# Where the first layer's projection stands, and how often it is halved, in two attention blocks in float32

## The chip, the cores and the metric

The kernel runs on one core of a Trainium2 chip. The metric is the device time of one execution in microseconds. PE is TensorE, DVE is VectorE, ACT is ScalarE, POOL is GpSimd, and SP is the engine whose queue issues most of the DMAs.

## The reference

There are 8 images of C = 512 channels and T = 1024 points, all in float32. Layer 0 has 8 heads of 64 channels, layer 1 has one head of 512.

```python
# layer 0
h = group_norm(x, 32 groups)
q, k, v = w_qkv @ h + b_qkv                       # 8 heads x 64
a = v @ softmax(k^T q / 8) , head by head
x = x + w_proj @ a + b_proj
# layer 1
h = group_norm(x, 8 groups)
q, k, v = q_w @ h + q_b, k_w @ h + k_b, v_w @ h + v_b
a = v @ softmax(q^T k / sqrt(512))
x = x + p_w @ a + p_b
```

## The kernel before

All products are float32 matmuls on PE. In layer 1 the weights of q and k are multiplied together once at the start (the product m) and so are those of v and p (the product z), so that an image needs g = m h, the scores h^T g, and z h times the exponentials.

**Halving.** A product of two matrices that are cut into quarters takes seven products of quarters in place of eight (Strassen's scheme in Winograd's form). `by_channel` and `by_token`, by way of `wino`, do this once: the seven factors of the image side are sums of halves of h (`image_factors`: eight differences of 128x512, in the tiles t1, t2, t4 and in place), those of the weights lie ready in DRAM (`keep`). `conv2` does it twice: each of the seven products is again cut into seven. For that the image side needs inner differences as well: `inner_factors` (line 414) makes 28 of 128x256, four for each of the seven outer factors. `conv2` goes through its products in four pairs (1 and 5; 2 and 6; 7; 3 and 4); each pair runs through the steps 1, 6, 2, 5, 7, 3, 4 (`inner_steps`), and what a pair leaves is added up further in the next. Evacuations out of PSUM are copies by ACT (lines 452 and 462) and additions by DVE (lines 528 and 530); a few additions between finished parts are made by POOL in SBUF (`more`, line 535).

The steps 3 and 4 of a pair, or of a whole `wino`, do not run at once. They stand in a list, `tail`, and the next pair or product runs its own step 1 first and then the list (`finish`). So PE has the tail of one product to do while ACT copies what the first step of the next one needs.

**Stages of image b, from 1 to 6, in PE's order:**

1. `attention0(b)`: eight units (four pairs of heads, two halves of the points). In each, PE makes scores, ACT exponentials (line 651), DVE their running sums (line 655), PE the product with v; ACT copies it to the tile a. The sums become reciprocals by way of DRAM (`reciprocals`) and a is multiplied by them (line 684). Between units, lists of hooks (`extra`) hold work for the next stage: the loads and the normalisation of layer 1's h of image b-1, its differences t by DVE, and a's own differences.
2. `projection(b)`: p = w_proj a, halved once, 28 matmuls of 512 columns. Meanwhile POOL makes the 28 inner differences of h1 of image b-1. Each evacuation adds the residual x on DVE (line 964); the result is stored to DRAM (`spill`), and its statistics for the second norm follow.
3. `layer1_scores(b-1)`: g by `conv2` with m.
4. `scores1`, then z by `by_token`, then `values1(b-1)`. In the hooks of `values1`, `factors_ahead` loads the next image's input, has ACT apply the first norm (`apply`, line 135, four instructions of 128x1024) and POOL make the inner differences of this h0.
5. `values(b+1)`: v by `conv2` with tokens in the rows. Ahead of it, the image after next is loaded (tiles `ahead`), and its statistics (line 93) are taken by DVE from a list, `background`, from which each step of a product takes one or a few entries.
6. `keys_and_queries(b+1)`: k and q, by `conv2`.

The first and the last image are framed somewhat differently. Weights go through three buffers in SBUF (`wpool`), loaded in the order of the list `uses`. Instructions with `keep_in_program_order` keep their place; the others may be moved on their engine by a scheduler. Each engine runs its own instructions strictly in order and waits on semaphores of the others.

Of the kernel before, what the change touches and what calls it, by code (L numbers as in the profile page):

```python
# [15 lines left out]
P = 128  # L16
EPS = 1e-5
ORDER = (1, 5, 2, 6, 7, 3, 4)
NBIG = 32
# [10 lines left out]
def two_attention_blocks_kernel(  # L30
# [22 lines left out]
    ident = const.tile([P, P], F32, name="ident")  # L53
    make_identity(nc, ident)
    ones = const.tile([P, P], F32, name="ones")
# [115 lines left out]
    def main_path(ctx):  # L171
# [7 lines left out]
        taken = []  # L179
        spool = ctx.enter_context(tc.tile_pool(name="spill", bufs=2, space=bass.MemoryType.DRAM))  # L180
# [111 lines left out]
        wdram2 = {n: dram.tile([P, 7, 7, P], F32, name=f"sums2_{n}") for n in "qkmv"}  # L292
# [21 lines left out]
        uses = ["p", *layer0] if B > 1 else ["p"]  # L314
        for b in range(1, B):
            uses += ["p", *twice["m"], "z"] + (layer0 if b + 1 < B else [])
# [86 lines left out]
        def inner_factors(hf, uid, pin=lambda ins: ins):  # L403

            f, steps = {}, []
            for p in ORDER:
# [5 lines left out]
                def make(ops=((t1, b12, b11), (t2, b22, t1), (t3, b22, b12), (t4, b21, t2))):  # L412
                    for dst, x, y in ops:
                        pin(nc.gpsimd.tensor_tensor(dst, x, y, ALU.subtract))  # L414
# [171 lines left out]
        def reciprocals(totals, uid, across, direct=None):  # L586
# [8 lines left out]
            for t in range(n):  # L595
                for i in range(4):
                    matmul(
                        sums[ts(i, 32), t, :, :], ones[:, :32], totals[t][:, :, ts(i, P)],
                        start=t == 0, stop=t == n - 1, skip_group_check=True,
                    )  # L600
# [31 lines left out]
        def attention0(b, q, k, v, a, extra):  # L632
# [3 lines left out]
            for hp in range(KC):  # L636
                for tb in (0, 1) if hp < KC - 1 else (1, 0):
# [35 lines left out]
                    if hp < KC - 1:  # L673
# [5 lines left out]
                    r = reciprocals(totals, uid, False, nc.scalar if (hp, tb) == (KC - 1, 0) else None)  # L679
                    totals = []  # L680
                    engine = nc.gpsimd if (b == 0 or hp == KC - 1) and (hp, tb) != (KC - 1, 0) else nc.vector
# [4 lines left out]
                    ]  # L686

            assert not extra
            return scaled[0]
# [118 lines left out]

        def natural(wt, nm, banks):
# [3 lines left out]
            for kc in range(KC):  # L813
                for o in range(KC):
                    transpose(pt[o][:, ts(kc, P)], wt[kc][:, ts(o, P)], ident)
# [36 lines left out]
        def prologue():  # L852
            raw_k = raw("k", 5)
# [46 lines left out]
            for n in "pz":  # L900
                t, steps = prepare(n)
                later.append(steps)
                later.append([lambda n=n, t=t: keep(n, t), load_weight])
# [86 lines left out]

        def norm_hooks(norm, uid):
# [16 lines left out]
        def keys_and_queries(b, f, norm, hooks):  # L1008
# [8 lines left out]
            else:  # L1017

                k = conv2("k", f, None, f"k0_{b}", [[all_background, *mean], [], [], affine])
                q = conv2("q", f, pcols("bq0"), f"q0_{b}")  # L1020
            return q, k

        def layer1_scores(b, inner):
            g = conv2("m", inner, ubias, f"g1_{b}")
# [29 lines left out]

        for b in range(B):
# [4 lines left out]
            h, loads, applies = [], [], []  # L1060
            if b > 0:
                h, loads, applies = begun(load_again, norm1, b - 1, "h1")
            elif B > 1:
                h, loads, applies = begun(load_x, norm0, 1, "h0")
            for f in loads:
# [3 lines left out]
            a = channel_tiles(f"a0_{b}")  # L1069

            here = lambda *t: tc.keep_in_program_order(nc.vector.tensor_sub(*t))
            af, steps = image_factors(a, f"a_{b}", here)

            if b > 0:
                hf, t = image_factors(h, f"h1_{b - 1}", here)
                for i, fs in enumerate((t[:1], t[1:2], (t[2], t[4]), (t[6], t[3]), (t[5], t[7]), steps[:2], steps[2:4])):
                    extra[2 * i + 3] += fs
            elif B > 1:
                hf, t = image_factors(h, "h0_1", here)
# [4 lines left out]
            if B > 1:  # L1084
                for f in steps[4:7]:
                    f()
            psum_pools(f"products_{b}", 2)
            xt = [load_x(b, c, "x") for c in range(KC)]
            if B > 1:

                inner, sums2 = inner_factors(hf, f"h1_{b - 1}" if b > 0 else "h0_1", tc.keep_in_program_order)
                for f in sums2:
                    f()
# [236 lines left out]
```

## Time and profile before

| | us |
|---|---|
| median of 3 runs | 2828.46 (2828.2 to 2830.94) |
| profiled execution | 2828.69 |
| its span | 2826.9 |
| period of a middle image (attention at 675.87, 1021.33) | 345.4 |
| projection p of that image, on PE | 792.62 to about 817.6 |
| g | from 817.62 |
| last product of layer 1 (`values1`) | 899.96 to 956.25 |
| v, k, q of the next image, from v's second step | 956.09 to 1021.26 |

The profile is of one execution. The mean clock granted to PE is 0.999 of the full one. A timeline's line has the start, the duration, the engine, the line of the kernel, the operation, out<-in by the tiles' names without their numbers, the shape, the count, and in brackets the idle time before it with what ended it. A float32 matmul of the program makes two records. Records overlap, so that PE's pace is read from starts.

### The profile page before, as it was taken

The page shows a single profiled execution, that of the slowest core. Times are in us where ns is not written, and L with a number is a line of the kernel's source. Part 1 is how long each engine was busy: PE and PEld are TensorE (multiplying, and loading weights), DVE is VectorE, ACT ScalarE, POOL GpSimd, SP SyncE. Part 2 cuts the span into 40 slices and gives each one's busy share as a digit, 9 for nine tenths or more (in the row PEclk, how much of TensorE's full clock was granted, in tenths as well). Part 3 has the DMA queues.
Part 4 walks back from the last instruction along what each step waited for, and adds up shares of the span by engine and source line. Part 5 has one row for each costly group of instructions (what it writes and reads, how often), then busy time and mean ns, then how long its engine had stood idle before and what let it go on. Part 6 is the DMA issues. An engine that isn't in the chain of part 4 may idle for free.

```text
span 2826.9 us, 33696 instructions
## 1 busy us (share of the span) xinstructions
PE 2808.6 (99%) x12434; PEld 1693.5 (60%) x12434; DVE 2005.0 (71%) x2833; ACT 942.7 (33%) x1205; POOL 1099.4 (39%) x1131
## 2 busy tenths in 40 slices
PE   9999999999999999999999999999999999999998
PEld 5435735866367653677537674376843868338584
DVE  5478677776777767777677766777667776676765
ACT  1252452214522145221552215422154312633130
POOL 2204205841057410664107730177202672036672
PEclk9999999999999999999999999999999999999999
DMA  8634303043031330323212232123311224112301
GB/s 285 209 114 151 147 17 127 27 174 139 24 139 52 147 129 17 139 98 120 110 50 105 101 138 90 53 102 122 140 67 53 102 112 159 36 58 90 119 5 72
DMA packets 107344, 292.41 MB, mean 103 GB/s; under 512 B 19171, under 2 KB 51235, under 8 KB 97446
## 3 DMA queue, kind: packets, MB, share of 16 engines
q1 hardware_dynamic: 105382, 287.92, 28.8%
q10 hardware_dynamic: 1792, 2.29, 0.3%
q8 instruction: 100, 1.64, 0.2%
q14 instruction: 70, 0.57, 0.1%
HBM read 237.47 MB, written 52.70 MB: 103 GB/s over the span
## 4 chain that ended last, share of the span: by engine, by line
PE 96%; DVE 2%; issue 1%; DMA 0%; POOL 0%; ACT 0%; DVEq 0%; ACTq 0%; POOLq 0%
PE sc L62 16%; PE av L62 15%; PE psb_av L62 6%; PE psb L62 5%; PE psa_av L62 4%; PE psc_av L62 4%; PE psc L62 3%; PE psa L62 3%; PE psb_z L62 3%; PE psb_k L62 3%; PE psb_g L62 3%; PE psb_v L62 3%; PE psb_p L62 3%; PE psb_q L62 2%; PE psa_z L62 2%; PE psc_z L62 2%
## 5 line engine op out<-in xcount | busy, mean ns | idle before, releaser
L655 DVE TENSOR_TENSOR sum<-sum,e 128x1024 f32<-128x1024 f32 x384 | 483.9, 1260 | 37.4 <-ACT e L651 0.5
L651 ACT ACTIVATE e<-sc 128x1024 f32<-128x1024 f32 x512 | 476.0, 1054 | 75.8 <-PE sc L62 74.2
L62 PE MATMUL sc<-q,k 64*128 64x512 f32 x2048 | 456.8, 596 | 0.0
L62 PE MATMUL av<-e,v 128*64 128x512 f32 x2048 | 453.6, 595 | 0.0
L684 POOL TENSOR_TENSOR a<-a,r 128x512 f32<-128x512 f32 (+1 forms) x11 | 20.0, 1817 | 903.3 <-DMA r<-all_rows 771.0
L62 PEld LDWEIGHTS sc<-q,k 64*128 64x128 f32 x2048 | 191.6, 186 | 248.0 <-issue 110.6
L62 PEld LDWEIGHTS av<-e,v 128*64 128x64 f32 x2048 | 141.3, 137 | 304.4 <-issue 292.3
L653 DVE TENSOR_TENSOR sum<-e,e 128x1024 f32<-128x1024 f32 x64 | 78.4, 1225 | 166.5 <-ACT e L651 166.5
L669 ACT COPY a<-av 128x512 f32<-128x512 f32 x64 | 37.5, 586 | 321.9 <-PE av L62 321.9
L62 PE MATMUL psb<-inner,inner_h 128*128 128x256 f32 x448 | 116.1, 382 | 0.9
L62 PE MATMUL psa_av<-e,z 128*128 128x512 f32 x256 | 113.3, 595 | 0.0
L414 POOL TENSOR_TENSOR inner_h<-h,inner_h 128x256 f32<-128x256 f32 x120 | 111.6, 931 | 3.5
L135 ACT ACTIVATE h<-h,b,s 128x1024 f32<-128x1024 f32 x62 | 78.5, 1270 | 87.1 <-DMA h<-in_x 69.4
L414 POOL TENSOR_TENSOR inner_h<-h 128x256 f32<-128x256 f32 x60 | 64.6, 1076 | 83.6 <-ACT h L135 83.6
L62 PEld LDWEIGHTS psb<-inner,inner_h 128*128 128x128 f32 x448 | 83.9, 190 | 16.6 <-POOL inner L429 3.5
L462 ACT COPY psb_v<-psa_v 128x512 f32<-128x512 f32 (+1 forms) x28 | 14.5, 517 | 222.4 <-DVE o L785 141.5
L725 POOL TENSOR_TENSOR sum<-sum,e 128x1024 f32<-128x1024 f32 x32 | 76.1, 2378 | 27.4 <-ACT e L721 26.1
L62 PE MATMUL psb_g<-inner_h,w_m 128*128 128x256 f32 x336 | 86.0, 383 | 0.3
L414 POOL TENSOR_TENSOR inner_h<-t_h,inner_h 128x256 f32<-128x256 f32 x90 | 84.2, 935 | 2.4
L414 POOL TENSOR_TENSOR inner_h<-t_h 128x256 f32<-128x256 f32 x90 | 79.9, 894 | 9.7 <-DVE t_h L165 9.7
L62 PEld LDWEIGHTS psa_av<-e,z 128*128 128x128 f32 x256 | 48.0, 190 | 57.3 <-issue 56.6
L721 ACT ACTIVATE e<-e 128x1024 f32<-128x1024 f32 x64 | 65.8, 1053 | 48.5 <-DVE e L711 26.2
(358 smaller groups left out, 5574.8 us busy)
## 6 DMA issues: line engine op xcount, KB each, us to landing
x<-in_x SPq DMA_DIRECT2D x36, 512.0 KB
h<-in_x SPq DMA_DIRECT2D x32, 512.0 KB
r<-all_rows SPq DMA_DIRECT2D x64, 256.0 KB
spill<-x SPq DMA_DIRECT2D x32, 512.0 KB
h<-spill SPq DMA_DIRECT2D x32, 512.0 KB
x<-spill SPq DMA_DIRECT2D x32, 512.0 KB
out<-x SPq DMA_DIRECT2D x64, 256.0 KB
w_p<-sums_p SPq DMA_DIRECT2D x8, 1792.0 KB
```

The lines of the kernel that those rows point to most:

```text
L62: tc.keep_in_program_order(nc.tensor.matmul(*args, **kw))
L135: tc.keep_in_program_order(nc.scalar.activation(dst, src, AF.Identity, bias=b, scale=s))
L414: pin(nc.gpsimd.tensor_tensor(dst, x, y, ALU.subtract))
L462: nc.scalar.copy(ps["b"], ps["a"])
L651: nc.scalar.activation(e, sc, AF.Exp, scale=(C // 8) ** -0.5)
L653: nc.vector.tensor_add(total, es[0], e)
L655: nc.vector.tensor_add(total, total, e)
L669: nc.scalar.copy(dst, av)
L684: engine.tensor_tensor(dst, dst, r, ALU.mult)
L721: nc.scalar.activation(e[c, cc, r], e[c, cc, r], AF.Exp, scale=scale)
L725: on = lambda dst, x, y: lambda: tc.keep_in_program_order(nc.gpsimd.tensor_tensor(dst, x, y, ALU.add))
```

## The change

For images 1 to 6:

- The projection leaves its place behind attention and stands between `values1(b-1)` and `values(b+1)`. It is halved twice (`projection2`, by `conv2`), for which the twice-halved sums of its weights are kept in DRAM too (`keep2`).
- Until then its input a waits in DRAM (`kept`): it is stored from attention pair by pair once it has been multiplied by the reciprocals, and loaded into the tiles `again` in the hooks of `values1`, where POOL makes its inner differences in the place where it made those of h0.
- The last two half units of attention have their reciprocals made together, and the last multiplication of a, by DVE, stands in g's second hook.
- The inner differences of h1 are made by DVE, in attention.
- The loads of h0 are issued behind `values1`'s code; its normalisation by ACT, its differences t and its inner differences by POOL stand in the hooks of the projection's four pairs.
- The residual is added by four separate additions of 128x1024 on DVE, in the hooks of v's first two pairs, and `spill` is stored behind them. The statistics of the second norm go to the background of k, and its means and factors to q.

There are 34 big tiles in place of 32; `ones` is narrower, and `ident` lies in a big tile. Images 0 and 7 keep the old way.

```diff
-NBIG = 32
+NBIG = 34
...
-        wdram2 = {n: dram.tile([P, 7, 7, P], F32, name=f"sums2_{n}") for n in "qkmv"}
+        wdram2 = {n: dram.tile([P, 7, 7, P], F32, name=f"sums2_{n}") for n in "qkmvp"}
...
-        uses = ["p", *layer0] if B > 1 else ["p"]
-        for b in range(1, B):
-            uses += ["p", *twice["m"], "z"] + (layer0 if b + 1 < B else [])
+        uses = ["p", *layer0]
+        for b in range(1, B - 1):
+            uses += [*twice["m"], "z", *twice["p"], *layer0]
+        uses += ["p", *twice["m"], "z"]
         uses += [*twice["m"], "z"]
...
-        def inner_factors(hf, uid, pin=lambda ins: ins):
+        def inner_factors(hf, uid, pin=lambda ins: ins, engine=nc.gpsimd):
...
-                        pin(nc.gpsimd.tensor_tensor(dst, x, y, ALU.subtract))
+                        pin(engine.tensor_tensor(dst, x, y, ALU.subtract))
...
-        def attention0(b, q, k, v, a, extra):
+        def attention0(b, q, k, v, a, extra, store=None):
...
-                for tb in (0, 1) if hp < KC - 1 else (1, 0):
+                for tb in (0, 1) if hp < KC - 1 or store else (1, 0):
...
-                    if hp < KC - 1:
+                    if hp < KC - 1 or store:
...
+                    if store:
+                        scaled.append(lambda hp=hp: store(hp))
...
+        def projection2(b, inner, hooks):
+
+            norm = GroupNorm(1, f"1_{b}")
+            y = conv2("p", inner, obias[0], f"p_{b}", hooks)
+            xt = [load_x(b, c, "x") for c in range(KC)]
+
+            def residual(c):
+                nc.vector.tensor_add(xt[c], xt[c], y[c])
+
+            def store():
+                spills[b] = spool.tile([KC, P, T], F32, tag="spill", name=f"spill_{b}")
+                for c in range(KC):
+                    nc.sync.dma_start(spills[b][c], xt[c])
+
+            stats = [lambda c=c: norm.stats(c, xt[c]) for c in range(KC)]
+            return norm, stats, [lambda c=c: residual(c) for c in range(KC)], store
...
-                k = conv2("k", f, None, f"k0_{b}", [[all_background, *mean], [], [], affine])
-                q = conv2("q", f, pcols("bq0"), f"q0_{b}")
+                _, _, mean1, affine1 = norm_hooks(norm1, f"1_{b - 1}")
+                k = conv2(
+                    "k", f, None, f"k0_{b}", [[all_background, *mean], [lambda: background.extend(stats)], [], affine]
+                )
+                q = conv2("q", f, pcols("bq0"), f"q0_{b}", [[all_background], mean1, affine1])
...
+            if 0 < b < B - 1:
+
+                inner, ih = inner_factors(hf, uid, tc.keep_in_program_order, nc.vector)
+                for i, fs in enumerate((
+                    t[:1], (t[1], ih[0]), (t[2], t[4]), (t[6], t[3], ih[1]), (t[5], t[7], ih[2]), ih[3:5], ih[5:],
+                )):
+                    extra[2 * i + 3] += fs
+                kept = apool.tile([KC, P, T], F32, tag="kept", name=f"kept_{b}")
+                psum_pools(f"attention_{b}", 1)
+                scaled = attention0(b, q, k, v, a, extra, lambda hp: nc.sync.dma_start(kept[hp], a[hp]))
+                psum_pools(f"products_{b}", 2)
+                gf, gsteps = layer1_scores(b - 1, inner, [[], scaled])
+
+                again = [None] * KC
+
+                def load_a(c):
+                    again[c] = big_tile(f"again_{b}_{c}")
+                    nc.sync.dma_start(again[c], kept[c])
+
+                ahead, made = factors_ahead(
+                    again, [lambda c=c: load_a(c) for c in range(KC)], [lambda: None] * KC, f"a_{b}"
+                )
+                layer1_rest(b - 1, inner, gf, gsteps, [], [[]] * 4, ahead)
+                h, loads, applies = begun(load_x, norm0, b + 1, "h0")
+                for f in loads:
+                    f()
+                hf, t = image_factors(h, f"h0_{b + 1}")
+                inner, ih = inner_factors(hf, f"h0_{b + 1}")
+                norm1, stats, sums, store = projection2(b, made["inner"], [
+                    [*applies, ih[0], *t[:2]], [ih[1], *t[2:4], ih[2]], [ih[3], *t[4:6], ih[4]],
+                    [ih[5], *t[6:], ih[6]],
+                ])
+                v, norm0 = values(b + 1, inner, [sums[:2], sums[2:], [store]])
+                q, k = keys_and_queries(b + 1, inner, norm0, (), norm1, stats)
+                continue
```

## The prediction

> **What bounds the kernel now.** I read the page's busy times and chain first, then the groups, then the timelines of one middle image (attention from 675.87 us, the next from 1021.33 us: a period of 345.4 us).
>
> ```profile
> span 2826.9 us, 33696 instructions
> PE 2808.6 (99%) x12434; PEld 1693.5 (60%) x12434; DVE 2005.0 (71%) x2833; ACT 942.7 (33%) x1205; POOL 1099.4 (39%) x1131
> PE 96%; DVE 2%; issue 1%; DMA 0%; POOL 0%; ACT 0%; DVEq 0%; ACTq 0%; POOLq 0%
> ```
>
> PE is busy for 99% and makes 96% of the chain. So a matmul removed is time gained, and any wait put in front of PE is time lost; there is almost no idle time left to win elsewhere (2826.9 - 2808.6 = 18 us).
>
> The Trainium skill (Trainium Kernel Development and Optimization, section Performance Expectations) calls matmul busy time a bad metric, since matmuls are pipelined, and would read the 60% of PEld: then fewer matmuls need not mean less time, and the gain below would be anything from 0 to its full size. The next rows speak for the full size.
>
> The timeline of PE has the projection (p) followed by g, the m product:
>
> ```profile
> 792.62 3.70 PE L62 MATMUL psa_p<-a,w_p 128*128 128x512 f32 x8
> 796.16 3.60 PE L62 MATMUL psc_p<-t_a,w_p 128*128 128x512 f32 x8
> ...
> 817.62 1.03 PE L62 MATMUL psb_g<-inner_h,w_m 128*128 128x256 f32 x4
> 818.48 0.59 PE L62 MATMUL psa_g<-h,w_m 128*128 128x256 f32 x2
> ```
>
> Starts matter, not durations: eight records take 799.59 - 796.16 = 3.43 us, four of the narrow ones 818.48 - 817.62 = 0.86 us. A program matmul of 512 columns is two records (0.859 us), one of 256 columns two records of half the length (0.43 us).
>
> The timelines of ACT, POOL and DVE show the work that the change puts beside p:
>
> ```profile
> 919.30 5.06 ACT L135 ACTIVATE h<-h,b,s 128x1024 f32<-128x1024 f32 x4 [11.65 <-DMA h<-in_x]
> ...
> 1003.00 0.58 ACT L452 COPY c_q<-psc_q 128x512 f32<-128x512 f32 x1 [0.28 <-PE psc_q L62]
> 1004.73 0.57 ACT L462 COPY psb_q<-psa_q 128x512 f32<-128x512 f32 x1 [1.14 <-PE psa_q L62]
> ```
> ```profile
> 799.71 0.72 POOL L414 TENSOR_TENSOR inner_h<-h,inner_h 128x256 f32<-128x256 f32 x1
> ...
> 814.25 1.17 POOL L414 TENSOR_TENSOR inner_h<-t_h,inner_h 128x256 f32<-128x256 f32 x1
> ...
> 971.13 0.72 POOL L535 TENSOR_TENSOR v<-v 128x256 f32<-128x256 f32 x1
> ```
> ```profile
> 746.40 1.22 DVE L684 TENSOR_TENSOR a<-a,r 128x1024 f32<-128x1024 f32 x1
> 747.54 1.29 DVE L1071 TENSOR_TENSOR t_h<-h,t_h 128x512 f32<-128x512 f32 x2
> ...
> 959.96 0.69 DVE L530 TENSOR_TENSOR v<-psb_v,c_v 128x512 f32<-128x512 f32 x1 [1.47 <-PE psb_v L62]
> 960.57 1.28 DVE L93 BATCH_NORM_STATS2 bnst<-ahead 128x6 f32<-128x512 f32 x2
> 961.76 0.68 DVE L530 TENSOR_TENSOR v<-psc_v,u_v 128x512 f32<-128x512 f32 x1
> ```
>
> The reader should take from them: four applies hold ACT for 5.06 us (1.27 each); POOL's difference of 128x256 takes 0.72 us alone and 1.17 us beside some of DVE's work; DVE starts the next instruction 1.14 us after a 128x1024 one, 0.60 us after a statistic or a 512-wide addition.
>
> **Removed from PE.** Once-halved, p has 28 matmuls of 512 columns: 28 x 0.859 = 24.05 us. Twice-halved it has 49 of 256 columns: 49 x 0.4294 = 21.04 us, which is also what q takes from its first psb step to the next attention (1000.22 to 1021.26). Gain 3.0 us an image, six images (1 to 6; 0 and 7 keep the old p): 18 us.
>
> **g behind attention.** Until now the last two steps of p stood between g's first step and its second and hid ACT's copy psb<-psa. Now nothing is left there: 0.57 us of copy and two handovers of 0.1 make 0.78 us. The last product a<-a,r (1.14 us of DVE) now stands among g's additions; I take 0.87 us of it as met by PE. Bounds: 0 (if DVE is idle there) and 0.78 + 1.14, plus some 2 us more if r comes late: its way over DRAM takes about 9.7 us from the sums to the landing (763.45 to about 773), and it has 1.6 us to spare. I take 1.65 us.
>
> **p and v in their new place.** T0 is when PE starts p's second step. This is the term that decides, and it is a chain through three engines' queues, each in program order.
> - ACT: behind the copy c5 (which ends at T0 + 3.36, as in q from 1000.22 to 1003.58) stand the four applies of the next image's h0; only then comes pair 1's copy psb<-psa. PE, which would start pair 1's second step at T0 + 6.0 (q: 1000.22 to 1006.25), gets it at about T0 + 9.1. This 3.1 us is overtaken by the next link and not added.
> - POOL: its 28 inner differences of h0 start with the first apply, at T0 + 3.36 + 1.27 = T0 + 4.65. Among them stand p's own 8 additions ("more"), the first of them only the 23rd of these 36 instructions, the last the 36th. DVE's additions of p's last pair wait for them. The pitch of 36 is the open number: 0.72 us alone; 27.3 / 28 = 0.975 us in values1 (920.62 to 947.9). The row nearest in kind is beside the old p, where DVE adds out of PSUM as it will here: nineteen from 799.71 to 815.42, 0.827 us. So the 36th ends at T0 + 4.65 + 29.8 = T0 + 34.4.
> - DVE: then the last addition of p (0.1 + 0.33), four residual additions x<-x,p (4 x 1.14 = 4.56), six statistics of the image ahead (6 x 0.60) with three aggregates (0.45), and only behind them v's first two evacuations (0.60 + 0.69, handover 0.1): 10.4 us. PE's fourth product of v's first pair needs the second of these.
> - So PE gets there at T0 + 44.8. Undisturbed it would be there at T0 + 21.04 + 5.36 = T0 + 26.4 (v: 956.09 to 961.45). The wait is **18.4 us** an image. With 0.72 it is 14.5, with 0.975 and DVE's pitch of 1.31 in its long sums 24.5.
>
> The Trainium skill (SBUF — State Buffer, section Who interferes with whom) calls the shared ports an exclusive lock: a DVE instruction with two SBUF inputs contends with GpSimd, one with a PSUM input does not. The trace half agrees: POOL runs at 0.72 beside v's PSUM additions, but beside DVE's SBUF sums at 1.17, not blocked for good. By the rule alone p's eight t differences would each hold POOL for 0.60, 36 x 0.72 + 8 x 0.60 = 30.7 us, an estimate that would put the total 6 us higher.
>
> **Costed at nothing.** The inner differences of h1 go to DVE in attention: 28 x 0.33 = 9.2 us (0.33 from the 256-wide additions that start at 969.15, 969.48 and 969.81), less a's eight differences that leave (4.8); DVE idles some 6.5 us in each of attention's four 29.2 us (such as 2.32, 2.54 and 1.67 before its rows at 737.28, 751.37, 763.45). If they didn't fit, the excess, up to 4 us an image, would delay av. a goes to DRAM and back, 2 MB each way on SP; a's factors take h0's place on POOL in values1; h0's loads are issued there some 25 us before T0, against 11 us for 4 MB (908.4 to 919.3). x and the ahead tiles queue on SP behind w_v's second half, which waits for pair 1's end (T0 + 14.7): 5.4 MB at that rate land by about T0 + 30, before DVE's place for them at T0 + 34.9; 3 us later costs 3. norm1's statistics, one per step of v and k (0.60 against PE's 0.86), are covered. The prologue's four more POOL additions and stores lie beside image 0's attention.
>
> **Sum.** -3.0 + 1.65 + 18.4 = +17.05 us an image, six times 102.3; image 6 has no image ahead of it for statistics, 4.0 less: +98.3. The profiled execution is 2828.69 us (1.8 us around its span), 0.2 us over the median: **2927 us**.
>
> **Rivals.** A, faster: nothing of the moved work reaches PE but the g term: 6 x (3.0 - 1.65) = 8 us less, 2820.6 (2810.7 without the g term). For it speaks POOL's low share, 39%. It decides where the 36th POOL instruction ends by T0 + 26.4 - 10.4 = T0 + 16.0, that is 0.32 us each; no row has POOL under 0.71. B: only p's own waits count, as v's evacuations get ahead of residual and statistics on DVE. The 30th POOL instruction ends at T0 + 29.5, PE's last step of p at T0 + 20.0 then waits to 30.3: 10.2 us; 6 x (-3.0 + 1.65 + 10.2) = +53, 2882. Against it: DVE takes them in the order above. C: contention as in values1 (0.975) or DMA late, 24.5 us: 6 x 23.15 - 4 = +135, 2964.
>
> **How the numbers follow.** Forecast 0.72 (its own range 2894 to 2950), B 0.09, C 0.11, A 0.08. The range runs from below B to C, 2872 to 2966. A 0.2% change (5.7 us) is about what this measurement can tell from none: faster 0.07, same 0.02, slower 0.91.
>
> **What would show it.** Right: PE idle at v's fourth product for 14 to 24 us in each of images 1 to 6, released by DVE, with POOL busy without a gap from p's fourth microsecond for some 30 us, ACT's copy of p's second pair behind the four applies, and p in 49 matmuls of 256 columns. Wrong: POOL done before v begins, DVE's residual behind v's evacuations, or new PE waits inside attention (av waiting for DVE) or on DMA of again, x or w_v.

## The result, and the profile after

| | before | after |
|---|---|---|
| median, us | 2828.62 (2828.2 to 2830.94, 4 runs) | 2938.37 (2929.98 to 2940.32, 4 runs) |
| profiled execution, us | 2828.69 | 2929.98 |
| its span, us | 2826.9 | 2928.1 |
| period of a middle image, us | 345.4 | 361.3 |

The ratio is 1.0381, 95% interval [1.0359, 1.0402]: the change costs 3.8%. The profiled execution happens to be the lowest of the four; the other three took 2937.07 to 2940.32 us.

The page of after, where the span, PE's busy time and the chain by engine stood before:

```profile
span 2928.1 us, 34809 instructions
PE 2827.0 (97%) x12686; PEld 1764.5 (60%) x12686; DVE 2069.2 (71%) x3091; ACT 974.7 (33%) x1265; POOL 1142.8 (39%) x1177
PE 84%; DVE 7%; POOL 5%; issue 3%; DMA 1%; ACT 1%; SPq 0%; DVEq 0%; ACTq 0%; POOLq 0%
```

The chain tells what the busy shares hide. POOL is at 39% as before, but PE's part of the chain has fallen from 96% to 84%, and DVE and POOL hold 12% of it. PE's busy time is even longer than before although the change removes matmul work: part of its records ran at a lower clock, as the windows below show for one image.

PE's waits in the whole span of after (who waited for whom: us in total, times, the longest):

```profile
PE psb_v L60 <- ACT psb_v L462: 23.2, 6, 3.9
PE psb_p L60 <- DVE u_p L530: 19.6, 12, 2.9
PE psb_p L60 <- ACT psb_p L462: 14.0, 6, 2.3
PE psb_v L60 <- DVE v L530: 9.7, 5, 3.2
PE tr_wk L63 <- DMA rawk<-in_w: 5.5, 1, 5.5
PE psb_g L60 <- DVE u_g L530: 4.5, 6, 0.8
PE psb_g L60 <- ACT psb_g L462: 4.3, 6, 0.7
PE sums L60 <- DVE sum L655: 3.7, 2, 3.0
```

Six images, so counts of 5, 6 and 12: four of these rows belong to p and v in their new place, two to g, one (sums) to image 0 and one (tr_wk) to the start of the kernel, where the kernel before has 3.6 us. The forecast was one long wait of PE at v's fourth product. In the image below that wait is only 1.62 us: p, which is held up too, waits on its way there, so that the delay comes as five waits of 11.9 us together, and PE runs part of the way at half its clock. The timeline of PE in the image whose attention starts at 335.89 us (only the lines that show a wait, in brackets):

```profile
601.51 1.10 PE L60 MATMUL psb_p<-inner_a,w_p 128*128 128x256 f32 x4 [2.33 <-ACT psb_p L462]
609.77 0.70 PE L60 MATMUL psb_p<-inner_a,w_p 128*128 128x256 f32 x2 [1.11 <-DVE u_p L530]
617.96 2.07 PE L60 MATMUL psb_p<-inner_a,w_p 128*128 128x256 f32 x4 [2.91 <-DVE u_p L530]
627.50 1.69 PE L60 MATMUL psb_v<-w_v,inner_h 128*128 128x128 f32 x8 [3.90 <-ACT psb_v L462]
636.35 2.05 PE L60 MATMUL psb_v<-w_v,inner_h 128*128 128x128 f32 x16 [1.62 <-DVE v L530]
```

The bracket of 627.50 names ACT. But ACT's copy psb_v started only at 626.78, because it stands in ACT's queue right behind ACT's own addition of the bias to p (626.16), and that one waited for POOL's last addition, which ended at 626.1. The three other engines' queues, in the same image:

```profile
596.25 4.64 ACT L133 ACTIVATE h<-h,b,s 128x1024 f32<-128x1024 f32 x4
600.79 0.58 ACT L462 COPY psb_p<-psa_p 128x512 f32<-128x512 f32 x1
...
626.16 0.72 ACT L542 ACTIVATE p<-p,obias 128x512 f32<-128x512 f32 x1 [1.45 <-POOL p L535]
626.78 0.58 ACT L462 COPY psb_v<-psa_v 128x512 f32<-128x512 f32 x1
```
```profile
597.56 1.24 POOL L414 TENSOR_TENSOR inner_h<-h 128x256 f32<-128x256 f32 x1 [10.87 <-ACT h L133]
...
616.40 0.72 POOL L535 TENSOR_TENSOR p<-p,p 128x256 f32<-128x256 f32 x1
...
625.40 0.73 POOL L535 TENSOR_TENSOR p<-p 128x256 f32<-128x256 f32 x1
```
```profile
617.15 0.76 DVE L530 TENSOR_TENSOR u_p<-psb_p,p 128x256 f32<-128x256 f32 x2 [4.04 <-POOL p L535]
...
626.16 0.48 DVE L528 SCALAR_TENSOR_TENSOR p<-psb_p,obias,p 128x256 f32<-128x256 f32 x1 [0.32 <-POOL p L535]
626.56 3.49 DVE L1008 TENSOR_TENSOR x<-x,p 128x1024 f32<-128x1024 f32 x3
...
635.05 0.65 DVE L530 TENSOR_TENSOR v<-psc_v,u_v 128x512 f32<-128x512 f32 x1
635.61 0.68 DVE L530 TENSOR_TENSOR v<-psb_v,c_v 128x512 f32<-128x512 f32 x1
```

Read from top to bottom: ACT's copy for pair 1 behind the four applies; 36 POOL instructions in a row, p's first own addition (line 535) as the 23rd at 616.40; DVE waiting 4.04 us for just that one; and v's second evacuation (635.61) behind residual and statistics. PE starts at 636.35, where this evacuation ends.

One thing here was not foreseen. PE's windows of the same stretch, cut where its granted clock changes (from:to, length, busy, records, granted clock, DMA share, GB/s):

```profile
614.24:617.66 3.42, 0.81 (x4) 1.00 1.03 416
617.66:621.07 3.41, 3.11 (x10) 0.50 1.03 414
621.07:624.48 3.41, 2.53 (x12) 1.00 0.09 35
624.48:627.90 3.42, 0.40 (x3) 1.00 0.97 327
627.90:631.31 3.41, 3.41 (x18) 0.50 0.97 358
631.31:634.72 3.41, 3.41 (x31) 1.00 1.01 407
```

Right after each of the two windows in which PE was busy for less than a quarter of the time, its granted clock is half for 3.41 us: the four records at 617.96 take 2.07 us, those at 601.51 only 1.10.

### The profile page after: what moved, and what is told of

The parts are those of the page before. It is cut to its first block, busy times and chain, and to the rows that moved or that the text cites. A ratio compares the mean times of both kernels' runs of the same rounds, so it can differ in the third digit from the quotient of the medians.

```text
span 2928.1 us, 34809 instructions
## 1 busy us (share of the span) xinstructions
PE 2827.0 (97%) x12686; PEld 1764.5 (60%) x12686; DVE 2069.2 (71%) x3091; ACT 974.7 (33%) x1265; POOL 1142.8 (39%) x1177
## 3 DMA queue, kind: packets, MB, share of 16 engines
q8 instruction: 102, 1.67, 0.2%
## 4 chain that ended last, share of the span: by engine, by line
PE 84%; DVE 7%; POOL 5%; issue 3%; DMA 1%; ACT 1%; SPq 0%; DVEq 0%; ACTq 0%; POOLq 0%
PE sc L60 14%; PE av L60 14%; PE psb_av L60 6%; PE psb L60 5%; PE psa_av L60 4%; PE psc_av L60 4%; PE psc L60 3%; PE psa L60 3%; PE psb_z L60 3%; POOL inner_h L414 3%; PE psb_k L60 3%; PE psb_g L60 2%; PE psb_q L60 2%; PE psb_v L60 2%; PE psa_z L60 2%
## 5 line engine op out<-in xcount | busy, mean ns | idle before, releaser
L655 DVE TENSOR_TENSOR sum<-sum,e 128x1024 f32<-128x1024 f32 x384 | 475.3, 1238 | 38.7 <-DVE sum L655 0.9
L535 POOL TENSOR_TENSOR g<-g,g 128x256 f32<-128x256 f32 x32 | 23.0, 730 | 835.3 <-DVE u_g L530 835.3
L60 PE MATMUL psb_v<-w_v,inner_h 128*128 128x128 f32 x588 | 81.8, 286 | 34.2 <-ACT psb_v L462 23.2
L60 PE MATMUL psb_p<-inner_a,w_p 128*128 128x256 f32 x252 | 72.8, 417 | 33.7 <-DVE u_p L530 19.6
L462 ACT COPY psb_p<-psa_p 128x512 f32<-128x512 f32 (+1 forms) x24 | 12.4, 519 | 268.6 <-DVE o L788 232.9
L60 PEld LDWEIGHTS psb_v<-w_v,inner_h 128*128 128x128 f32 x588 | 74.0, 198 | 40.5 <-issue 27.2
L685 POOL TENSOR_TENSOR a<-a,r 128x1024 f32<-128x1024 f32 (+1 forms) x5 | 12.0, 2408 | 198.9 <-DVE sum L655 149.5
L719 POOL TENSOR_TENSOR e<-e,e 128x512 f32<-128x512 f32 x64 | 80.6, 1270 | 19.9 <-DVE e L714 19.9
L714 DVE TENSOR_TENSOR e<-psc,u 128x512 f32<-128x512 f32 x56 | 38.6, 690 | 68.4 <-PE psc L60 68.4
```

Of the source, the lines that this page charges most:

```text
L60: tc.keep_in_program_order(nc.tensor.matmul(*args, **kw))
L462: nc.scalar.copy(ps["b"], ps["a"])
L535: nc.gpsimd.tensor_tensor(d, x, y, ALU.add)
L655: nc.vector.tensor_add(total, total, e)
L685: engine.tensor_tensor(dst, dst, r, ALU.mult)
L714: nc.vector.tensor_add(dst[0], ps, x[0])
```

## The experiments

**Theory.** An image of the new kind loses its time where POOL's queue of 36 (28 differences of the next image's h0, and between them p's own 8 additions) ends, plus what DVE has in front of v's evacuations. The rivals: DVE's order by itself; the new place by itself, however p is halved; ACT's applies; and something outside images 1 to 6. The kernel before was run along with each group: 2829.68, 2827.94, 2829.04, 2828.6 and 2828.63 us in the medians.

### ACT's applies earlier

```diff
-                for f in loads:
+                for f in loads + applies:
...
-                    [*applies, ih[0], *t[:2]], [ih[1], *t[2:4], ih[2]], ...
+                    [ih[0], *t[:2]], [ih[1], *t[2:4], ih[2]], ...
```

> ACT applies the norm of the next image's h0 right behind its loads, ahead of the projection's copies, and not between the projection's first and second pair. POOL's order stays. Theory (ACT's queue, then POOL's 36 instructions, then DVE's queue): POOL can begin when it is done with a's differences, some 6 us ahead of the projection's second step in place of 4.6 us behind it; its 36 instructions of 0.79 us then end at about T0 + 22, DVE's additions and statistics take 10 us more, and PE's fourth product of v waits 5 to 6 us in place of 17: 2850 to 2860 us. Rival 1 (only the copy that stands behind the applies matters): 2.5 us an image less than the changed kernel, about 2923. Rival 2 (DVE's residual and statistics bind by themselves, whenever POOL ends): no more than 20 us less.

Measured: 2915.93 us (2911.66 to 2918.59), ratio 1.0308 [1.0291, 1.0325]. That is far from 2850 to 2860. The wait of p's second step for ACT is gone, all others stay. POOL's timeline shows why (attention from 337.03, T0 = 594.10):

```profile
589.60 1.98 POOL L414 TENSOR_TENSOR inner_h<-h,inner_h 128x256 f32<-128x256 f32 x2
599.26 2.24 POOL L414 TENSOR_TENSOR inner_h<-t_h 128x256 f32<-128x256 f32 x2 [7.68 <-DVE t_h L163]
...
623.67 0.72 POOL L535 TENSOR_TENSOR p<-p 128x256 f32<-128x256 f32 x1
```

With h ready early, POOL gets through four differences and then stands for 7.68 us until DVE has made the first t_h, which is still in p's first hook. The 36th ends at T0 + 30.3 in place of T0 + 33.2, 2.9 us earlier, and the period is 358.47 us in place of 361.33, 2.9 us shorter. The edit failed at what it was meant to do. The time by itself does not separate the theory from its rivals: 22 us less is near both the first rival's 2923 us and the second's limit of 20 us. The trace does. PE's wait of 2.3 us for ACT's copy is gone, but at 616.24 PE still waits 2.23 us for an addition of DVE that POOL holds up. DVE's last addition of p is still released by POOL, and v's fourth product (634.63) comes 10.2 us after POOL's end, as in after (636.35 - 626.1). What POOL's end gains, the image gains.

### p's own additions first

```diff
-                    [*applies, ih[0], *t[:2]], [ih[1], *t[2:4], ih[2]], [ih[3], *t[4:6], ih[4]],
-                    [ih[5], *t[6:], ih[6]],
+                    [*applies, ih[0], *t[:2]], [ih[1], *t[2:4]], t[4:6], t[6:],
...
-                v, norm0 = values(b + 1, inner, [sums[:2], sums[2:], [store]])
+                v, norm0 = values(b + 1, inner, [[*ih[2:4], *sums[:2]], [ih[4], *sums[2:]], [*ih[5:], store]])
```

> Only 8 of the 28 inner differences of h0 stand in the projection's hooks; the other 20 follow in the hooks of v. So POOL makes the projection's own 8 additions as soon as their inputs are there. The applies stay where the changed kernel has them. Theory: the projection then runs as it should but for 2.5 us behind the applies; v's fourth product still waits some 5 to 6 us for DVE's residual additions and statistics: per image -3.0 + 0.9 + 2.5 + 5.6, about 2870 us with the 5 us that image 0 lost. Rival (POOL is not what the projection waits for): within 10 us of the changed kernel's 2930 to 2940.

Measured: 2908.98 us (2907.11 to 2910.48), ratio 1.0279 [1.0262, 1.0296]. p now runs without a wait except the one for ACT, so the order on POOL was what held it. But the time lies between theory (2870 us) and rival (2920 us or more): the remaining delay now stands at v's fourth product, where DVE is late. DVE, POOL and PE at that place:

```profile
620.63 5.01 DVE L1008 TENSOR_TENSOR x<-x,p 128x1024 f32<-128x1024 f32 x3
...
631.35 0.68 DVE L530 TENSOR_TENSOR v<-psb_v,c_v 128x512 f32<-128x512 f32 x1
```
```profile
621.19 1.71 POOL L414 TENSOR_TENSOR inner_h<-t_h,inner_h 128x256 f32<-128x256 f32 x1
622.87 1.70 POOL L414 TENSOR_TENSOR inner_h<-t_h 128x256 f32<-128x256 f32 x1
...
626.19 0.72 POOL L414 TENSOR_TENSOR inner_h<-h 128x256 f32<-128x256 f32 x1
```
```profile
632.09 3.78 PE L60 MATMUL psb_v<-w_v,inner_h 128*128 128x128 f32 x16 [7.00 <-DVE v L530]
```

The stack of residual and statistics still stands in front of v's evacuations (620.63 to 630.79), and beside POOL's differences a residual takes 1.67 us of DVE, against 1.16 in after (3.49 / 3), where POOL had just finished. After a wait of 7.00 us PE then runs sixteen records in 3.78 us; in the kernel before the same sixteen took 1.95.

### v's evacuations ahead of DVE's stack

```diff
-                        nc.vector.tensor_add(d, psi, xi)
+                        add_ = nc.vector.tensor_add(d, psi, xi)
+                        if by_tokens:
+                            tc.keep_in_program_order(add_)
...
-                nc.vector.tensor_add(xt[c], xt[c], y[c])
+                tc.keep_in_program_order(nc.vector.tensor_add(xt[c], xt[c], y[c]))
...
-                v, norm0 = values(b + 1, inner, [sums[:2], sums[2:], [store]])
+                v, norm0 = values(b + 1, inner, [[], sums[:2], sums[2:], [store]])
```

The statistics of the image ahead are also pinned, behind three empty entries of `background`.

> On DVE the evacuations of v's first pair keep their place ahead of the statistics of the image ahead and of the residual additions, which follow behind them. ACT's and POOL's orders stay. Theory: v's second step comes as late as before, 13.6 us, since that wait is POOL's; only the 3 us that v's fourth product waited more fall away, and the statistics cost 0 to 1 us in v's second pair: 12 to 20 us less, 2915 to 2926. Rival (the DVE queue's 9 us are what PE waits for): 50 us less, about 2885.

Measured: 2945.85 us (2943.41 to 2947.89), ratio 1.0413 [1.0396, 1.043], more than after itself. The wait at v's fourth product is gone from the list; new rows take its place:

```profile
PE psb_v L60 <- DVE u_v L530: 16.3, 18, 1.4
...
PE psc_v L60 <- DVE c_v L530: 5.6, 5, 1.1
```

The stack moved behind v's first pair and now gets in the way of v's other pairs. In the image whose attention starts at 337.78, PE also runs at half its clock from 621.18 to 634.83, four windows of 3.41 us in place of after's two. Rival B of the prediction priced this order at 2882 us. It had p's wait in its price, and this wait stays; but the stack is not free behind v's first pair, as B had it. The periods of images 1 to 5 are 362.0 to 364.8 us.

### p halved once, in the new place

`projection2` is replaced by the old `projection`'s code (`by_channel`), in the new place, with a's factors taken from the tiles `again`; no twice-halved sums of p's weights are made.

> The projection stands in its new place and its input waits in DRAM, but it is halved once, as before: 28 matmuls of 512 columns (24.05 us), no additions by POOL, residual in the evacuations; the twice-halved weights aren't made. The applies stand behind its first step. Theory (the twice-halved product's additions on POOL, queued among h0's differences, are what costs): 6 x 0.9 us for g plus at most 2 us an image, 2832 to 2846. Rival (the new place costs by itself, by DMA, residual or the later applies): 2870 or more.

Measured: 2871.25 us (2870.25 to 2872.78), ratio 1.0148 [1.0131, 1.0165]; the rival's number. 67 us of the 110 are back. The run changes several things at once: p has no additions on POOL, its residual is added in the evacuations and not in a stack, and POOL begins its 28 differences of h0 before p's second step. So the 67 us can't be put down to POOL's additions alone. What is left is mostly another wait, two times 2.0 to 2.2 us per image:

```profile
PE psc_p L60 <- DVE o L788: 23.9, 12, 2.2
```

The last evacuations of `values1` come late, and the banks of PSUM that they empty are those that p's second step wants. POOL has its part in that: beside its differences (1.17 us each) DVE's multiplications there take 1.21 us, against 0.69 in after.

```profile
588.86 1.21 DVE L789 TENSOR_TENSOR o<-o,r 128x512 f32<-128x512 f32 x1
```

So the next run only changes the order of p's steps:

```diff
-                weight("p"), af, f"p_{b}", residual, middle=(5, 6, 7, 2), ...
+                weight("p"), af, f"p_{b}", residual, middle=(6, 2, 5, 7), ...
```

> As the run with the projection halved once in the new place, but with its steps in the order 1, 6, 2, 5, 7 in place of 1, 5, 6, 7, 2, so that the PSUM banks that the last product's evacuations on DVE still hold are not wanted at once. There PE waited 2.04 and 2.15 us for these evacuations in each image. Theory (place alone costs about 1 us, those waits were the rest): 6 x 4.2 = 25 us less than 2871, so 2843 to 2850. Rival (the wait only moves to the next step, as DVE is late by itself): 2860 or more.

Measured: 2848.66 us (2847.1 to 2851.68), ratio 1.0071 [1.0055, 1.0086], as expected. The row is gone, and the period is 348.4 us. So the new place costs 3.0 us an image (348.4 against 345.4) with a p that is halved once; g's two waits (1.5 us) and a new wait of 1.0 us for DVE's w_p are in it. 13 of the 16 us come in with the twice-halved p and the orders it runs in.

### All queues reordered, p halved twice

The applies and the first two t directly behind the loads; four of the seven sets of differences in p's hooks and three in v's; v's evacuations pinned ahead of the residual, one residual in each of v's hooks; the statistics cut in halves and moved, for norm1 into k, for the image ahead into q.

```diff
+                for f in applies + t[:2]:
+                    f()
...
-                    [*applies, ih[0], *t[:2]], [ih[1], *t[2:4], ih[2]], [ih[3], *t[4:6], ih[4]],
-                    [ih[5], *t[6:], ih[6]],
+                    [ih[0], ih[1], *t[2:4]], [ih[2], *t[4:6]], t[6:], [ih[3]],
...
-                v, norm0 = values(b + 1, inner, [sums[:2], sums[2:], [store]])
+                v, norm0 = values(b + 1, inner, [[ih[4]], [ih[5], *sums[:1]], [ih[6], *sums[1:3]], [sums[3], store]], True)
```

> Twice-halved in the new place, with all three queues in another order: ACT applies the norm of h0 right behind its loads; DVE makes h0's first differences there too; POOL makes four of the seven groups of inner differences in the projection's hooks and the other three in v's; on DVE v's evacuations go ahead of the residual, which follows in v's second to fourth pair; the second norm's statistics go to k in halves, one in two steps, those of the image ahead to q. Theory (the 18 us an image are queue order, not work that PE must wait for): per image -3.0 + 0.9 + at most 2, with 5 us lost in image 0: 2820 to 2835. Rival (POOL and DVE are short of time in this stretch, whatever the order): 2870 or more.

Measured: 2842.0 us (2838.45 to 2845.08), ratio 1.0047 [1.0033, 1.006]; 7 us above the upper end of what I expected. The period is 345.23 us, so an image of the new kind is now no longer than one of before. Against the run with p halved once it is 3.2 us shorter (348.40 - 345.23), though the orders differ too. 96 us of 110 are back without a changed product: the new kind of image lost its time by the order of the queues. Of the four rows of p and v that led after's list of waits (66.5 us), 0.8 us is left.

Part of the difference is image 0: it takes 216.4 us from its attention to the next here, 211.2 and 209.5 in the two runs without twice-halved sums for p, and 210.6 before. These sums are four POOL additions of 128x896 that stand together beside DVE's running sums of the exponentials. In after: 10.30 us of POOL from 136.25, DVE's six sums from 141.68 in 11.27 us, where before they took 7.87, and PE's wait of 3.0 us for `sum` in the list above. The next run puts them into image 0's hooks one at a time, with their stores behind the last:

```diff
-                    later.append([lambda t=t: keep2("p", t)])
+                    later += [[f] for f in keep2("p", t, spread=True)]
```

> As the kernel with all three queues reordered, and in image 0 the four sums of 128x896 for the twice-halved projection weights stand one in each hook in place of four at once, their stores behind the last. Theory (these sums slow DVE's running sums at the end of image 0's second unit, where PE waited 2.97 us and then ran 1.6 us slower): 3 to 5 us less than the kernel without this. Rival (what image 0 loses is the queue of stores on SP): no gain, or a loss.

Measured: 2837.48 us (2833.61 to 2840.52), ratio 1.0034 [1.0022, 1.0047]: 4.5 us less. The ranges of the two runs overlap, but in the profiles image 0 is at 212.06 in place of 216.4. In the trace three of the four sums still run in a row (7.27 us from 135.97) and only the fourth comes later (164.91); DVE's six sums take 9.58 us in place of 11.27, and PE's wait is 1.26 us in place of 2.98. The stores moved along with the sums, so their share, the rival, is not tested by itself.

### g's two waits

What is left in the list of waits of that run in each of the six images:

```profile
PE psb_g L60 <- DVE u_g L548: 4.5, 6, 0.8
PE psb_g L60 <- ACT psb_g L480: 4.3, 6, 0.7
```

These are the two terms of the prediction's section on g. The cover that was taken from ACT's copy can be given back with other PE work:

```diff
+                        def close(totals=totals, uid=uid):
+                            last["r"] = reciprocals(totals, uid, False)
+
+                        def scale(dst=dst):
+                            tc.keep_in_program_order(nc.gpsimd.tensor_tensor(dst, dst, last["r"], ALU.mult))
+
+                        return [close, scale, lambda hp=hp: store(hp)]
...
+                tail.append(scaled.pop(0))
                 gf, gsteps = layer1_scores(b - 1, inner, [[], scaled])
```

> Everything of the image-0 run stays; new is the end of each attention: the eight sums products of the last pair of heads are issued behind the first step of g instead of ahead of it, and the last multiplication of a by r is GpSimd's instead of VectorE's. My theory: g's two waits per image there (4.5 and 4.3 us over six images, so 0.75 and 0.71 each) were waits with nothing queued to cover them, and the sums products cover them, so about 8.5 us less than the image-0 run's 2837.5: 2829, between 2826 and 2833, which is the time of the kernel before within a fifth of a per cent. Rival: the multiplication now ends later (GpSimd takes longer for it than VectorE) and g's additions on GpSimd queue behind it, so that the wait moves to g's second or third step and the time stays at 2835 to 2840.

Measured: 2831.8 us (2825.54 to 2833.63), ratio 1.0007 [0.9998, 1.0016]. That is in the theory's range. Both rows are gone and the period is 344.2 us, but a new one, of the rival's kind, stands first in the list:

```profile
PE psb L60 <- POOL inner L447: 5.9, 6, 1.0
```

> As the run before with the sums products behind g's first step, but the last multiplication of a by r stays VectorE's. In that run GpSimd's multiplication (2.35 us, at 466.30 in the image whose attention starts at 334.68) stood ahead of g's pair additions and of the next product's inner factors, and TensorE waited 0.98 us per image for those factors (5.9 us in six images). My theory: without it in that queue the wait goes and the period falls from 344.2 to about 343.2 us, so 2831.8 less 6: 2826, between 2823 and 2830, at or just under the time of the kernel before. Rival: VectorE's multiplication (about 1.2 us) now stands ahead of g's third evacuation and the wait returns there as one for u_g of 0.7 to 1 us per image; the time stays at 2830 to 2834.

Measured: 2835.69 us (2830.97 to 2837.41), ratio 1.0022 [1.0012, 1.0031], 1.7 us above even the rival's range. It is the rival's side: the multiplication takes DVE 1.64 us just where g's evacuations stand, and PE's wait is for c_g (3.9 us, 6 times). So the next run has the multiplication on POOL again, at another place:

```diff
-                6, 4, (1, 0), (1, 0), [], stats[10:] + add_up(1, 1) + add_up(0, 1), (),
+                6, 4, (1, 0), (1, 0), [], stats[10:] + add_up(1, 1) + add_up(0, 1) + late, (),
...
-                gf, gsteps = layer1_scores(b - 1, inner, [[], scaled])
+                gf, gsteps = layer1_scores(b - 1, inner)
+                late[:] = scaled
```

> As the run with the sums products behind g's first step and GpSimd's last multiplication of a by r, but that multiplication and its store stand behind the additions of layer 1's second exponentials in GpSimd's queue, where GpSimd sat idle for 2.51 us (519.98 to 522.49 in the image whose attention starts at 334.68), instead of ahead of g's additions. My theory: TensorE's 0.98 us per image for g's inner factors goes (5.9 us in six images) and nothing takes its place, since the stored part is loaded again only about 20 us later: 2826, between 2822 and 2830. Rival: with the multiplication away the next wait of the same kind shows (the factors' chain from g's evacuation is as long as before, and the other runs had 0.65 to 0.75 us here whatever was moved): 2829 to 2833.

Measured: 2827.76 us (2822.67 to 2830.0), ratio 0.9995 [0.9986, 1.0004]. POOL's timeline has the multiplication in the gap that was aimed at, and PE's waits for g and for its inner factors are gone:

```profile
517.74 2.39 POOL L706 TENSOR_TENSOR a<-a,r 128x1024 f32<-128x1024 f32 x1
520.29 5.64 POOL L758 TENSOR_TENSOR sum<-sum,e 128x1024 f32<-128x1024 f32 x2 [0.17 <-ACT e L754]
```

The period is 343.67 us, 0.5 less than 344.2 and not 1.0: the wait for DVE's e in the scores (3.2 us in seven images) is the next in the row. A next wait is what the rival had said, though its 2829 to 2833 us did not come. How much of the 4.0 us between the two medians belongs to the move stays open, because the profiled execution of the version with POOL's multiplication ahead of g lost about 5 us in its last image (428.9 us from the last attention to the end, against 424.1), where one DVE instruction was very slow (see the end).

This is the best version of the changed kernel, and it can't be told from the kernel before. By the two profiled executions images 1 to 6 gain 8.3 us ((2402.49 - 330.41) - (2396.73 - 333.00)), the start and image 0 lose 2.6, and the span is 6.1 us shorter (2820.8 against 2826.9). But that execution is the lowest of eleven: three took 2822.67 to 2823.38 us, the other eight 2826.86 to 2830.0. Where those eight lose their 5 us no profile shows; the slow pair of instructions at the end of this document costs about as much in the profiles that have it, which makes it a candidate and no more.

## Why the prediction was right, and where it was not

The time came out 11.4 us over the forecast (2938.4 against 2927), the sign and the range were right, and the cause was the one named. The shape was not: the prediction's own sign was PE idle for 14 to 24 us at v's fourth product, and PE is idle there for 1.62 us and for 11.9 us in five places. What the chain did fix is when that product starts. The working step by step, in the image with T0 = 592.97 (p's second step on PE):

| step | predicted | measured |
|---|---|---|
| pair 1's step behind the applies | T0 + 9.1 | 601.51 = T0 + 8.5 |
| POOL's first difference | T0 + 4.65 | 597.56 = T0 + 4.6 |
| pitch of the 36 | 0.827 | 28.6 / 36 = 0.79 |
| the 36th ends | T0 + 34.4 | 626.1 = T0 + 33.2 |
| DVE's stack up to v's second evacuation | 10.4 | 636.35 - 626.1 = 10.2 |
| v's fourth product | T0 + 44.8 | 636.35 = T0 + 43.4 |
| its delay against the predicted T0 + 26.4 | 18.4 | 17.0 |
| g | 1.65 | 0.75 + 0.71 = 1.46 in waits |
| matmuls | -3.0 | -3.2 (periods of two runs, p halved twice against once; their orders differ too) |

- **The chain.** The links of ACT, POOL and DVE that the prediction named hold, and their order was read from the order of instructions alone. One more came in: ACT's bias addition to p, which waits for POOL, ahead of ACT's copy for v. The largest error of size on the chain is the pitch, 0.79 for 0.827: POOL runs at 0.72 as soon as DVE's t differences are over, and mostly at 1.17 beside them.
- **The undisturbed way.** The prediction took p's 21.04 us from q's row as well (1000.22 to 1021.26). That was a coincidence: q's first four records stand ahead of 1000.22, and short pauses fill the place. In the reordered kernel, which has no wait above 0.1 us there, PE takes 27.05 us from p's second step to v's fourth product (594.60 to 621.65) and not 26.4. By that the delay is 16.3 us, and the removed matmuls gain 2.4 us in this place and not 3.0; the sum of the two is the same.
- **g.** The waits are as priced, but the image's offset at p grows less: v's second step came 280.29 us after the attention's start before (956.09 - 675.80); less p's 24.05 this is 256.24, and after has T0 at 592.97 - 335.89 = 257.08. So g's net cost is 0.84 us, about half of 1.65. PE even has a third new wait on this way, 0.46 us for DVE's e. About 0.45 us of what makes up for them has only moved: the second norm's two small products (gmean, gvar) stood ahead of p's new place before (888.42 and 895.55) and stand in q now. The rest is not traced. With both waits covered, in the reordered kernel, the period fell by 1.05 us (345.23 to 344.18), although a new wait of 0.98 came.
- **The sum per image.** The five periods of images 1 to 5 average (2144.70 - 335.89) / 5 - 345.4 = 16.4 us more than before, against 17.05. From the measured terms it would be 17.0 + 0.84 - 3.0 = 14.8; the image of the table has 15.9. The 1.1 us between lie behind v's fourth product: 0.6 us in v's second pair, where statistics of x (640.07 and 641.44) stand ahead of DVE's evacuation, and 0.45 us in q, where gmean and gvar now stand (685.23 and 689.56).
- **Image 6.** It is 2.8 us shorter than the others' average (358.93 against 361.76), not 4.0.
- **The step that failed** is the sentence "The prologue's four more POOL additions and stores lie beside image 0's attention", costed at nothing. Lying beside it was the price: image 0 takes 4.1 us more (214.66 against 210.6). The runs without these additions (211.2 and 209.5 us) and with them moved apart (212.06) show that this is mostly their work. Image 0's attention also starts 1.4 us later (121.23 against 119.81). That is not theirs: it starts at 121.04 and 121.87 in the two runs without them too, where the row tr_wk, a wait for a weight's DMA, has 5.3 and 5.2 us against 3.6 before; its cause stays open. A row of the right kind stood in the prediction's own fences, POOL at 1.17 in place of 0.72 (814.25) beside DVE's additions of SBUF tiles; it was read for POOL alone and not for DVE, which loses as well.
- **The rest of the miss.** The profiled execution, 2930, is 2.9 us over the forecast, and part of that closeness is luck: images 1 to 6 lose 95.7 us in place of 98.3, the start and image 0 the 5.5 us that were not priced. The other three runs of after lie 7 to 10 us higher. Two of them have a mean granted clock of 0.986 and 0.988, the third 0.990 as the profiled one; the kernel before is at 0.998 to 1.000 wherever it ran and spreads over 2.7 us here. So a slower clock can be part of the 7 to 10 us and not all of it, and no profile shows the rest.
- **Costed at nothing, rightly:** DVE's inner differences of h1 in attention, and the DMA of a, x and the ahead tiles: no PE wait of images 1 to 6 lies inside attention or is put down to a DMA.
- **The rivals.** A (nothing reaches PE) needed POOL's 36th by T0 + 16.0; it came at T0 + 33.2, and only the changed orders bring A's case about (periods of 345.2 to 343.7 us, where A has 344.0). B had waits in p, which are there, but its premise, that DVE's stack behind v's first evacuations costs nothing, is refuted by a run. C's contention does not happen in after, where residual and POOL are apart; the run with p's additions first brought them together and has it.

## What to carry to other kernels

A 39% busy helper engine can set the time: count how many of its instructions, in program order, stand between a result and the first one that somebody waits for, and multiply by a pitch from the trace. Put the few instructions that the critical engine waits for ahead of the many that are only needed later, and do this on every queue of the chain at once: to repair one queue moved the wait to the next (ACT to POOL, POOL to DVE, DVE to v's later pairs), and of the orders tried, only the one that changed all of them together gave back 96 of 110 us. When a piece of a tail that covered a copy is taken away, give the copy other cover in the same edit.

## What the runs showed of the hardware

**PE's clock after stalls.** In the windows of after shown above, the granted clock is 0.50 for 3.41 us each time that PE was busy for little of the 3.41 us before: 0.81 us ahead of 617.66, 0.40 us ahead of 627.90. The same wait at the same place shows that its length does not decide. ACT's copy for p's second pair costs PE 2.33 us in after and in the run with v's evacuations ahead of DVE's stack. In after it falls over two windows, with PE busy for 2.00 and 2.49 us, and no slow record follows. In the other run it falls into one:

```profile
600.70:604.12 3.42, 1.09 (x6) 1.00 0.00 0
604.12:607.53 3.41, 3.41 (x10) 0.50 0.00 0
```

The edge between half and full clock lies near 40% of a window in these runs: in the run with early applies one with 1.32 us busy (from 1688.14) is followed by half the clock, one with 1.45 us (from 2046.54) is not. The clock comes back after a busy window: from 621.18 in the run with v's evacuations ahead it stays at half through windows with 2.69, 2.62 and 1.87 us busy and returns after one with 3.41. The Trainium skill (TensorE: Matmul & The Clock Gate, Part 1) describes a gate that halves the clock after an idle window of about 3.4 us that runs freely, and gives it back after a busy one. Length, halving and the free-running window agree with it; but the window before need not be idle here, PE was busy in it for up to 1.32 us.

**DVE and POOL both lose.** DVE's residual x<-x,p (two inputs in SBUF) and POOL's difference take 1.67 and 1.70 us side by side (three pairs, in the run with p's additions first), 1.16 and 0.72 apart. Side by side each takes nearly the sum of the two, 1.88. The Trainium skill (SBUF — State Buffer, section Who interferes with whom) calls the shared ports an exclusive lock, and these pairs agree with it: their times add up, as if the two engines took turns.

**One instruction of seven microseconds.** In the last image of the first run on g's waits, one instruction of POOL and one of DVE took ten times as long as their like (0.72 and 0.69):

```profile
2647.72 7.30 POOL L432 TENSOR_TENSOR inner_h<-h,h 128x256 f32<-128x256 f32 x1 [0.58 <-ACT h L133]
```
```profile
2664.84 7.80 DVE L819 TENSOR_TENSOR o<-o,r 128x512 f32<-128x512 f32 x1
```

PE then waits 3.3 us for w_av. The same two instructions stand out (6.9 to 7.8 us) in five of the twelve profiles: in this run, in the one with p's additions first, in the two with p halved once and in the first reordered one. In these five the time from the last attention to the end is 428.9 to 430.5 us, in the other seven 424.1 to 425.4. The cause is not shown.
